# Values once per pixel, and key rows that rotate through six places: a change to an attention and convolution kernel

## The chip, the cores and the metric

The kernel runs on one core of one Trainium2 chip. The metric is the device time of one execution in microseconds (us). A core has a matrix engine (TensorE, PE in the profile), three engines for elementwise work (VectorE = DVE, ScalarE = ACT, GpSimd = POOL), and SyncE (SP), which issues most of the DMA transfers. Each engine works through its own list of instructions in order, and they meet at semaphores. On-chip memory is SBUF (128 partitions); TensorE writes to PSUM, in banks of 512 floats per partition, and another engine must copy a bank out before it is used again.

## The reference

Two layers over x of shape (2, 128, 256, 256), float32, NCHW, each added to its own input. `_gn` is a group norm with 32 groups over a whole image.

```python
x = x + attention(_gn(x))     # layer 0
x = x + conv_block(_gn(x))    # layer 1
# attention: windows of 8x8 queries, neighbourhoods of 12x12 keys and values
q, k, v = split(einsum('bchw,oc->bohw', x, W_qkv), 3)    # 4 heads of 32
k, v = unfold_windows(k), unfold_windows(v)              # padded by 2, step 8
attn = einsum('bnd,bmd->bnm', q * SCALE, k)
attn = softmax(attn + rel_pos_emb(q, rel_height, rel_width) + FIXED_MASK)
out = einsum('bnm,bmd->bnd', attn, v)                    # then W_out, 1x1
```

FIXED_MASK leaves only pairs of pixels whose relative position has one fixed parity in the rows and one in the columns. So a window falls into four classes (r, c) of row and column parity, in each of which 16 queries meet 6 x 6 = 36 keys, and no pair crosses between them. The conv block is a 5x1 convolution and a 3x1 depthwise one, times a dilated 1x3 projection to 8 channels.

## The kernel before, in words

**Tiling.** An image is 32 strips of 8 rows, and the strips of both images are counted k = 0 to 63. Layer 0 works in units u = 2k + r: the row parity r of strip k, 128 units. A unit covers 32 windows of one strip as 16 pairs of neighbours, both column parities c. For a pair and one (r, c), the keys are a block of 6 rows x 10 columns = 60 (two 6 x 6 neighbourhoods that overlap by two columns), on 60 of 64 partitions; c = 0 and c = 1 take the two halves of the 128.

**Order.** The order of each engine's list is written by hand: what the main loop calls in sequence is what TensorE, VectorE, ScalarE, GpSimd and SyncE each run in sequence. One unit is:

- SyncE: the rows of strip k+2 (`load_rows`, in even units), a load of later rows for the next image's group norm statistics (`load_next`, in odd units), and the unit's result rows (`f_x1`, in `project`, to DRAM).
- VectorE, in even units: `normalise(k + 1)`, which writes the normed rows (L343) into padded cells `xn` of 60 elements, together with what neighbours share: the last two rows of the strip before (L334, GpSimd) and the edge columns (L348, L349). In odd units: `input_stats`.
- GpSimd: `by_place` (L358) sorts the pixels of strip k+1 into `xq`, and `old_keys` (L369) moves the two key rows that two strips share from one key buffer to the other.
- TensorE: `biases` (L479), which writes relative position logits and the mask to the four score banks; `scores` (L495); `values` (L460), which projects one padded cell per product, 16 products a unit; `coefficients` for the next strip (L439); `attend` (L520); then, in even units, `keys` of two later units (L375), in odd ones `queries` of two later units (L414); and `project` (L375 again, f_py).
- ScalarE and VectorE copy out of PSUM: exponentials (L504), values (L466, eight copies a unit), coefficients (L448 and L452), keys (L388), queries (L420), and the division of `attend`.

A value product's 128 result rows are the 60 padded places of c = 0 and of c = 1, so that a bank can be copied straight to `vt`, the operand of `attend`. A pixel at a strip's or a pair's edge lies in more than one cell, and is projected for each.

**Buffers.** `ps_pj` has four PSUM banks, in rotation for all products but the scores. `xn` has two buffers, by strip; `kt` two for each r; `vt` has one; the result rows `x1` two; rows of x (`raw`) three, and the statistics loads (`sx`) one. Layer 1 begins when layer 0's last units end, and takes over its buffers.

## Time and profile before

| | us |
|---|---|
| median of 3 runs (lowest, highest) | 3065.4 (3065.05, 3065.92) |
| the profiled execution: its own time | 3064.28 |
| its span on the profiler | 3062.5 |
| busy: TensorE matmuls | 2954.8 |
| busy: VectorE | 2517.6 |
| busy: ScalarE | 1732.8 |
| busy: GpSimd | 654.4 |

The span is a little shorter than the execution's own time, by 1.8 us, which lies around it. The page gives busy time of each engine, the chain of work that ended last, and groups of instructions by line. A line of a group reads: line, engine, operation, what is written <- what is read, tile shapes and count, then busy time, mean length of one in ns, and idle time ahead with its releaser. A line of a timeline reads: start in us, length, engine, source line, operation; "x32" says that 32 instructions were merged into one line; what stands in square brackets is idle time ahead and who ended it. TensorE's records are pipelined: a mean length of one counts overlaps, and the time from one start to the next is the better measure.

### The profile page before, as it was taken

To read this page: it belongs to the slowest core of one execution; us is meant where nothing else is said; L and a number is where in the kernel's file an instruction comes from. 1 tells how busy PE (TensorE), PEld (TensorE's weight loads), DVE (VectorE), ACT (ScalarE), POOL (GpSimd) and SP (SyncE) were. 2 spreads that over 40 slices of the span, in tenths; PEclk is the share of its full clock that TensorE was granted. 3 is DMA by queue.
4 is the path that set the end of the run, shared out by engine and by line. 5 is a ranking of instruction groups with operands and counts; after the bars stand their busy time and mean duration, and the time that the engine had idled before them with its cause. 6 is when DMAs were issued, how large, how long until landed. Compare 5 with 4: busy or idle time off the path is not lost.

```text
span 3062.5 us, 116727 instructions
## 1 busy us (share of the span) xinstructions
PE 2954.8 (96%) x52100; PEld 2224.4 (73%) x52100; DVE 2517.6 (82%) x4107; ACT 1732.8 (57%) x2677; POOL 654.4 (21%) x1437
## 2 busy tenths in 40 slices
PE   0799999999999999999999999999999999999998
PEld 0688888888888888888888888884444444444443
DVE  8788888888888877777777777768999999999997
ACT  0455555555555656555555555556666665666664
POOL 2323232323232323232323232310000000000000
PEclk9999999999999999999999999999999999999999
DMA  9433333333333222222222222226888888888885
GB/s 393 176 123 123 116 116 113 116 113 117 113 116 113 85 72 89 72 89 72 89 72 89 72 89 72 86 84 160 214 219 218 215 210 220 215 218 218 219 216 157
DMA packets 137407, 434.88 MB, mean 142 GB/s; under 512 B 12992, under 2 KB 87744, under 8 KB 104640
## 3 DMA queue, kind: packets, MB, share of 16 engines
q1 hardware_dynamic: 127824, 361.24, 34.0%
q0 software_dynamic: 9072, 66.06, 11.8%
q8 instruction: 413, 6.77, 0.9%
q14 instruction: 98, 0.80, 0.1%
HBM read 284.65 MB, written 134.22 MB: 137 GB/s over the span
## 4 chain that ended last, share of the span: by engine, by line
PE 95%; DVE 0%; ACT 0%; POOL 0%; DMA 0%; issue 0%; SPq 0%; ACTq 0%
PE f_pv L460 16%; PE a_o L783 11%; PE a_e L783 11%; PE f_s L495 8%; PE f_o L520 8%; PE f_pq L414 8%; PE f_pk L375 8%; PE f_py L375 7%; PE f_pa L439 4%; PE f_s L479 4%; PE a_d L834 4%; PE b L876 2%; PE a_c L783 2%; PE g L763 2%; POOL f_xq L358 0%; DMA ident<-in_c_ident 0%
## 5 line engine op out<-in xcount | busy, mean ns | idle before, releaser
L466 DVE COPY f_vt<-f_pv 64x512 f32<-64x512 f32 x512 | 354.7, 695 | 289.3 <-ACT f_vt L466 289.3
L358 POOL COPY f_xq<-f_xn 128x128 f32<-128x128 f32 x1024 | 397.9, 440 | 697.5 <-DVE f_xn L343 669.9
L460 PE MATMUL f_pv<-f_wqkvT,f_xn 128*128 128x128 f32 x4096 | 491.3, 278 | 0.0
L460 PEld LDWEIGHTS f_pv<-f_wqkvT,f_xn 128*128 128x128 f32 x4096 | 466.9, 192 | 8.5
L504 ACT ACTIVATE f_p<-f_s 128x512 f32<-128x512 f32 x512 | 264.4, 603 | 320.4 <-PE f_s L495 320.4
L420 ACT ACTIVATE f_q<-f_pq,f_head 128x512 f32<-128x512 f32 x512 | 302.8, 703 | 139.6 <-PE f_pq L414 139.6
L466 ACT COPY f_vt<-f_pv 64x512 f32<-64x512 f32 x512 | 297.6, 583 | 117.3 <-PE f_pv L460 116.8
L858 ACT ACTIVATE t<-t,w 128x1024 f32<-128x1024 f32 x127 | 145.9, 1149 | 367.6 <-DVE t L851 362.8
L865 DVE SCALAR_TENSOR_TENSOR t<-t,w,t 128x1024 f32<-128x1024 f32 x254 | 325.8, 1283 | 7.4 <-ACT t L858 1.3
L495 PEld LDWEIGHTS f_s<-f_q,f_kt 64*64 64x64 f32 x16384 | 250.8, 135 | 49.9 <-issue 49.9
L495 PE MATMUL f_s<-f_q,f_kt 64*64 64x64 f32 x16384 | 268.5, 220 | 0.6 <-issue 0.6
L388 ACT COPY f_kt<-f_pk 128x512 f32<-128x512 f32 x256 | 154.5, 604 | 196.6 <-PE f_pk L375 196.6
L520 PE MATMUL f_o<-f_vt,f_p 128*32 128x66 f32 x16384 | 262.4, 222 | 0.2 <-issue 0.2
L894 POOL DMA_DIRECT2D y<-f_x x63 | 54.6, 866 | 916.0 <-DVE y L886 612.5
L520 PEld LDWEIGHTS f_o<-f_vt,f_p 128*32 128x32 f32 x16384 | 241.1, 110 | 9.2 <-issue 0.3
L783 PE MATMUL a_o<-xm,w1s 128*128 128x512 f32 x512 | 241.7, 593 | 3.8 <-ACT t L774 3.8
L375 PE MATMUL f_pk<-f_xn,f_wqkvT 128*128 128x128 f32 (+2 forms) x1256 | 244.2, 346 | 0.0
L375 PE MATMUL f_py<-f_ot,f_woT 128*128 128x256 f32 x1024 | 242.0, 379 | 0.9 <-DVE f_ot L538 0.9
L783 PE MATMUL a_e<-xm,w1s 128*128 128x512 f32 x512 | 240.7, 591 | 0.0
L414 PE MATMUL f_pq<-f_xq,f_wq_s 128*128 128x256 f32 (+1 forms) x1370 | 240.6, 331 | 0.0
L334 POOL COPY f_xn<-f_xn 128x1280 f32<-128x1280 f32 x62 | 87.1, 1404 | 717.2 <-PE f_pv L460 717.2
L414 PEld LDWEIGHTS f_pq<-f_xq,f_wq_s 128*128 128x128 f32 x1370 | 208.3, 191 | 22.6
(141 smaller groups left out, 4701.1 us busy)
## 6 DMA issues: line engine op xcount, KB each, us to landing
f_raw<-in_x SPq DMA_DIRECT2D x62, 1280.0 KB, 7.8
f_x<-f_x SPq DMA_DIRECT2D x128, 512.0 KB, 3.4
y<-f_x POOLq DMA_DIRECT2D x63, 1024.0 KB, 8.0
out<-y SPq DMA_DIRECT2D x63, 1024.0 KB
f_sx<-in_x SPq DMA_DIRECT2D x54, 1024.0 KB, 12.0
raw<-f_x SPq DMA_DIRECT2D x64, 640.0 KB, 6.8
raw<-f_x SPq DMA_DIRECT2D x62, 384.0 KB, 7.4
f_sx<-in_x SPq DMA_DIRECT2D x8, 1280.0 KB
```

Source lines behind the costliest of these rows:

```text
L358: nc.gpsimd.tensor_copy(xq[:, half, t2, :, :, c].rearrange("p t r n e -> p r t n e"), cells[:, :, 16 * half + c : 16 * half + 16 : 2, 1 + ...
L375: nc.tensor.matmul(dst[:, 512 * lo // last : 512 * hi // last], w, moving[:, n * lo // last : n * hi // last], start=True, stop=True,)
L388: nc.scalar.copy(cur[:, c, 1:129, 2:6], pk.rearrange("p (j i) -> p j i", i=4))
L414: nc.tensor.matmul(pq.rearrange("p (h n e t) -> p h t n e", h=2, n=8, e=2)[:, half, lo:hi], wq_s, xq[:, half, :, :, r, c].rearrange("p s t ...
L420: nc.scalar.activation(q[:, c, :, i], pq.rearrange("p (n x) -> p n x", n=NPAIR), AF.Copy, scale=head[:, i : i + 1],)
L460: nc.tensor.matmul(pv[:, P * n : P * n + P], xn[k % 2][:, r, 4 * j + n].rearrange("p c x -> p (c x)"), wvT, start=True, stop=True,)
L466: (nc.vector.tensor_copy if c else nc.scalar.copy)(vt[rows, 4 * j : 4 * j + 4, :, c, 0:32], pv[rows].rearrange("p (n h d) -> p n h d", n=4 ...
L495: nc.tensor.matmul(sc[g][n // 8][64 * c : 64 * c + 64, n % 8].rearrange("p i x -> p (i x)"), keys_k[rows, c, 48 * n : 48 * n + 64], qs[u][ ...
L504: nc.scalar.activation(pts[u][:, g, 8 * half : 8 * half + 8].rearrange("p n i x -> p (n i x)"), sc[g][half].rearrange("p n i x -> p (n i x ...
L520: nc.tensor.matmul(po[32 * h : 32 * h + 32, n - lo], p[:, h // 2, n, h % 2], vt[:, n, h], start=True, stop=True,)
L783: nc.tensor.matmul(pa[:, : n * W], w, rows, start=i == 0, stop=i == len(terms) - 1)
L865: nc.vector.scalar_tensor_tensor(t3[:, j : j + 4], t1[:, j + tap : j + tap + 4, :], w3[:, tap : tap + 1], t3[:, j : j + 4], ALU.mult, ALU.add,
```

## The change

A strip's values are projected once per pixel. `xn` now holds, for each pair, the 128 pixels of four rows of each parity (r, c, row i, column j), only the four rows that the strip brings new; a small `xo` keeps the row that the queries need besides. `values(k + 1, ...)` does all 16 pairs in two halves, one in each unit of strip k: two banks a unit, one copied out by ScalarE and one by VectorE, into `vn`, which has a single buffer, in pixel order.

`bring(r, ...)` then copies `vn` by DMA, on SyncE's queue, from SBUF to SBUF into key order in `vt[r]`: for each c and piece one copy of the strip's own pixels and two of the edge columns that go to the neighbouring pairs. Both calls stand in the odd unit, `bring(0)` after the values, `bring(1)` after `attend`. Strip 0 of an image has two further rows above (`top_values`, built like `values`, and `bring_top`), held in the buffer `sx`.

Keys and values keep the rows that two strips share in place. The six key rows have six slots, and a strip's four new ones overwrite the four oldest: slots 2 to 5, 0 to 3, then 4, 5, 0, 1, and again. In the third case (k mod 3 = 2) the run wraps and is two pieces. A row keeps its slot, so the table `hot` of `biases` has three phases, by k mod 3. `old_keys` goes; `beside` (GpSimd) copies the edge columns of the keys. `kt` and `vt` are one buffer for each r, and `x1` one in place of two.

The norm is done a unit earlier, in odd units for strip k+2, the statistics in even ones, `by_place` after the keys or queries. Queries read `xn` and `xo`. The products of keys, queries and projections are cut into pieces by the table `PIECES`, and the first three or four halves of `biases` are cut in two. In layer 1 the pixel buffers take over the place of `vn` (`pixel_buffers`).

The core of the diff ("..." stands for lines left out, among them the removed bodies):

```diff
...
-ONE, TWO, THREE = (0, 32), (0, 16, 32), (0, 16, 24, 32)
-XC = 131
+ONE, TWO, THREE, FOUR = (0, 16), (0, 8, 16), (0, 6, 11, 16), (0, 4, 8, 12, 16)
+NKEY = 60
+PIECES = {
+    0: (ONE, ONE, ONE, 0), 1: (ONE, ONE, TWO, 0), 60: (THREE, TWO, THREE, 1), 62: (TWO, TWO, TWO, 0),
+    64: (THREE, TWO, THREE, 1), 70: (THREE, TWO, THREE, 1),
+}
...
+        xt = [both.sb.tile([P, 12 * 260], F32, tag=f"x{i}", name=f"f_xn{i}") for i in range(2)]
+        xn = [t[:, 0:2048].rearrange("p (n r c i j) -> p n r c i j", n=NPAIR, r=2, c=2, i=4) for t in xt]
+        xo = [t[:, 2048:2560].rearrange("p (n r c j) -> p n r c j", n=NPAIR, r=2, c=2) for t in xt]
+        tops = {}
+        kt = [cst.tile([P, 2, NPAIR * NKEY + 4], F32, tag=f"f_kt{r}", name=f"f_kt{r}") for r in range(2)]
+        vt = [cst.tile([P, NPAIR, 2, HEADS, 33], F32, tag=f"f_vt{r}", name=f"f_vt{r}") for r in range(2)]
+        vn = both.sb.tile([P, NPAIR, HEADS, 33], F32, tag="vn", name="f_vn")
...
-        x1p = l0.enter_context(tc.tile_pool(name="f_x1", bufs=2))
+        x1p = l0.enter_context(tc.tile_pool(name="f_x1", bufs=1))
...
+        def pieces(u):
+            return PIECES.get(u, (THREE, TWO, THREE, 4 if u % 4 == 1 else 3))
...
+            for i in range(NS - 3):
+                n = 10 if i < 12 else 8
+                stats_at[2 * (b * NS + i) + 2] = b + 1, row, n
...
+            for i, u in enumerate((16, 28, 44, 58)):
...
+            norm_at[2 * (b * NS + NS - 2)] = st_x, b + 1, f"x{b + 1}"
+            norm_at[2 * ((b + 1) * NS + 3)] = st_y, b, f"y{b}"
...
+        def slots_of(k):
+            first = (4 * k + 2) % 6
+            return [(0, 4, first)] if first < 4 else [(0, 2, 4), (2, 2, 0)]
         def normalise(k):
...
+            cur = xn[k % 2]
+            rows = raws[k].rearrange("p (i r) (n j c) -> p r c n i j", r=2, n=NPAIR, c=2)
...
+                t = rawp.tile([P, 10, W], F32, tag="sx", name=f"f_top_{k}", bufs=1).rearrange("p a b -> p (a b)")
+                x = t[:, 0:1024].rearrange("p (n r c i j) -> p n r c i j", n=NPAIR, r=2, c=2, i=2)
+                v = t[:, 1024 : 1024 + 8 * HEADS * 33].rearrange("p (n h d) -> p n h d", n=8, h=HEADS)
...
+                tops[b] = t[:, 0:1024], x, v
+                for r in range(2):
+                    nc.vector.tensor_scalar(
+                        x[:, :, r, :, 1], rows[:, r, :, :, 0].rearrange("p c n j -> p n c j"), mean, rstd,
+                        ALU.subtract, ALU.mult,
+                    )
+                before = x[:, :, :, :, 1]
...
+                before = xn[(k + 1) % 2][:, :, :, :, 3]
+            nc.gpsimd.tensor_copy(
+                xo[k % 2].rearrange("p n r c j -> p n (r c) j"),
+                before.rearrange("p n r c j -> p n (r c) j"),
+            )
...
+                        cur[:, :, r, c, 0 : hi - 1], rows[:, r, c, :, 1:hi], mean, rstd,
...
         def by_place(k, columns):
...
+            lo, hi = columns
+            for half in range(2):
+                windows = slice(8 * half, 8 * half + 8)
+                for c in range(2):
+                    nc.gpsimd.tensor_copy(
+                        xq[:, half, lo:hi, 0, :, c].rearrange("p t r n e -> p r t n e"),
+                        xo[k % 2][:, windows, :, c].rearrange("p n r (e t) -> p r t n e", t=4)[:, :, lo:hi],
+                    )
+                    for t2 in range(lo, hi):
...
+                            xq[:, half, t2, 1:4, :, c].rearrange("p t r n e -> p r t n e"),
+                            xn[k % 2][:, windows, :, c, 0:3, t2:8:4].rearrange("p n r i e -> p r i n e"),
...
+        def by_window(r):
+            return kt[r][:, :, 0 : NPAIR * NKEY].rearrange("p c (n x) -> p c n x", x=NKEY)
+        def beside(r, slot, m):
+            keys_r, end = by_window(r), NPAIR - 1
+            for side, dst, src, j in ((0, slice(1, NPAIR), slice(0, end), 7), (1, slice(0, end), slice(1, NPAIR), 0)):
+                first = 48 + 2 * slot + side
+                nc.gpsimd.tensor_copy(
+                    keys_r[:, :, dst, first : first + 2 * m - 1 : 2],
+                    keys_r[:, :, src, 8 * slot + j : 8 * (slot + m) : 8],
+                )
         def keys(u, first=TWO, second=TWO):
...
+            keys_r = by_window(r)
             def part(c):
...
+                in_parts(second if c else first, pk, wkT, xn[k % 2][:, :, r, c].rearrange("p n i j -> p n (i j)"))
+                for i, m, slot in slots_of(k):
+                    nc.scalar.copy(
+                        keys_r[:, c, :, 8 * slot : 8 * (slot + m)],
+                        pk.rearrange("p (n x) -> p n x", n=NPAIR)[:, :, 8 * i : 8 * (i + m)],
+                    )
+                if c:
+                    for i, m, slot in slots_of(k):
+                        beside(r, slot, m)
             def top():
...
+                beside(r, slot, 2)
...
+        def queries(u, first=TWO, second=TWO):
...
             def part(c):
...
+                by_pair = pq.rearrange("p (n x) -> p n x", n=NPAIR)
...
+                nc.tensor.matmul(by_pair[:, :, 0:8], wq_s, xo[k % 2][:, :, r, c], start=True, stop=True)
...
+                        by_pair[:, lo:hi, 8:32], wq_s,
+                        xn[k % 2][:, lo:hi, r, c, 0:3].rearrange("p n i j -> p n (i j)"),
...
+                        q[:, c, :, i].rearrange("p n (j t) -> p n j t", t=4),
+                        pq.rearrange("p (n t j) -> p n j t", n=NPAIR, t=4), AF.Copy,
...
+        def values(k, groups):
+            for g in groups:
+                pv = ps_pj.tile([P, 512], F32, tag="pj", name=f"f_pv_{k}_{g}")
+                for n in range(4):
+                    nc.tensor.matmul(
+                        pv[:, P * n : P * n + P],
+                        xn[k % 2][:, 4 * g + n].rearrange("p r c i j -> p (r c i j)"),
+                        wvT, start=True, stop=True,
+                    )
+                (nc.vector.tensor_copy if g % 2 else nc.scalar.copy)(
+                    vn[:, 4 * g : 4 * g + 4, :, 0:32], pv.rearrange("p (n h d) -> p n h d", n=4, h=HEADS)
+                )
+        def top_values(b):
...
+        def bring(r, pieces):
+            end = NPAIR - 1
+            for c in range(2):
+                at, to = 32 * (2 * r + c), 64 * c
+                for i, m, slot in pieces:
+                    lo = at + 8 * i
+                    nc.sync.dma_start(
+                        vt[r][to + 8 * slot : to + 8 * (slot + m), :, c], vn[lo : lo + 8 * m]
+                    )
+                    first = to + 48 + 2 * slot
+                    nc.sync.dma_start(
+                        vt[r][first : first + 2 * m - 1 : 2, 1:NPAIR, c], vn[lo + 7 : lo + 8 * m : 8, 0:end]
+                    )
+                    nc.sync.dma_start(
+                        vt[r][first + 1 : first + 2 * m : 2, 0:end, c], vn[lo : lo + 8 * m - 7 : 8, 1:NPAIR]
+                    )
+        def bring_top(r, b):
+            v, slot = tops[b][2], 4 * NS * b % 6
+            for c in range(2):
+                for odd in range(2):
+                    lo, to = 64 * odd + 16 * (2 * r + c), 64 * c
+                    nc.sync.dma_start(
+                        vt[r][to + 8 * slot : to + 8 * slot + 16, odd:NPAIR:2, c], v[lo : lo + 16]
+                    )
+                    first = to + 48 + 2 * slot
+                    nc.sync.dma_start(
+                        vt[r][first : first + 3 : 2, odd + 1 : NPAIR : 2, c], v[lo + 7 : lo + 16 : 8, 0 : 8 - odd]
+                    )
+                    nc.sync.dma_start(
+                        vt[r][first + 1 : first + 4 : 2, 1 - odd : NPAIR - 1 : 2, c],
+                        v[lo : lo + 9 : 8, 1 - odd : 8],
+                    )
+        def biases(u, halves=0):
...
+            done = 0
...
+                            for lo, hi in ((0, 4), (4, 8)) if done < halves else ((0, 8),):
+                                nc.tensor.matmul(
+                                    sc[g][half][
+                                        64 * c : 64 * c + 64, lo:hi, :, 16 * e : 16 * e + 16
+                                    ].rearrange("p n i x -> p (n i) x"),
+                                    hot[rows, k % 3, e],
+                                    cfs[k][rows, e, r, c, lo:hi].rearrange("p n i x -> p n (i x)"),
+                                    start=e == 0 and lo == 0, stop=False, skip_group_check=True,
+                                )
+                            done += 1
         def scores(u):
...
+                            kt[r][rows, c, NKEY * n : NKEY * n + 64],
...
+                            vt[r][:, n, :, h], start=True, stop=True,
...
-                in_parts(TWO, py, woT, ots.pop((u, c)).rearrange("p (n x) -> p n x", n=NPAIR))
+                in_parts(pieces(u)[2], py, woT, ots.pop((u, c)).rearrange("p (n x) -> p n x", n=NPAIR))
...
         load_rows(0)
         load_rows(1)
-        load_next()
         weights.load()
         with tc.manual_schedule(engines=ORDERED):
             normalise(0)
-            by_place(0, range(4))
-            emit(keys(0, ONE, TWO))
+            emit(keys(0, ONE, ONE))
+            top_values(0)
+            bring_top(0, 0)
+            values(0, range(4))
+            for r in range(2):
+                bring(r, slots_of(0))
+            bring_top(1, 0)
+            by_place(0, (0, 4))
             coefficients(0, 0)
             coefficients(0, 1)
+            normalise(1)
+            by_place(1, (0, 2))
             for u in range(2):
-                emit(queries(u, TWO, TWO))
+                emit(queries(u, ONE, ONE))
             for u in range(NU):
                 k, r = divmod(u, 2)
                 b, s = divmod(k, NS)
...
                 if r == 0:
                     if k + 2 < NB * NS:
                         load_rows(k + 2)
-                    if more:
-                        normalise(k + 1)
+                elif k + 2 < NB * NS:
+                    normalise(k + 2)
                 if u in stats_at:
                     input_stats(u)
+                if u == 0 or u in stats_at:
                     load_next()
...
-                if more:
-                    by_place(k + 1, (2 * r, 2 * r + 1))
...
-                if later:
-                    old_keys(u + 1)
-                biases(u)
+                biases(u, pieces(u)[3])
                 scores(u)
...
-                for j in range(4):
-                    values(u, j)
+                if more:
+                    at_top = (k + 1) % NS == 0
+                    if at_top and r == 0:
+                        top_values(b + 1)
+                    values(k + 1, (2 * r, 2 * r + 1))
+                    if r == 1:
+                        bring(0, slots_of(k + 1))
...
                 attend(u)
+                if more:
+                    if at_top:
+                        bring_top(r, b + 1)
+                    if r == 1:
+                        bring(1, slots_of(k + 1))
...
                 turn(u)
...
                 if r == 0:
-                    top = s == 0 or (k + 1) % NS == 0
-                    if u == 0:
-                        emit(keys(1, ONE, ONE))
-                    else:
-                        emit(keys(u + 1, TWO if top else THREE))
+                    emit(keys(u + 1, pieces(u)[0], pieces(u)[0]))
                     if more:
-                        emit(keys(u + 2, ONE if u > 0 and top and s else TWO if top else THREE))
+                        emit(keys(u + 2, pieces(u)[0], pieces(u)[0]))
                 elif later:
-                    second = THREE if k % 4 else TWO
-                    emit(queries(u + 1, THREE, TWO) + queries(u + 2, THREE, second))
+                    emit(queries(u + 1, pieces(u)[1], pieces(u)[1]) + queries(u + 2, pieces(u)[1], pieces(u)[1]))
+                if more and r == 0:
+                    by_place(k + 1, (2, 4))
+                elif k + 2 < NB * NS:
+                    by_place(k + 2, (0, 2))
                 if u > 0:
                     result_stats(u - 1)
                 project(u)
...
         def rows_buffer(i):
...
+            t = both.sb.tile([P, 12 * 260], F32, tag=f"x{i}", name=f"xm{i}")
+            xn[i] = t.rearrange("p (r w) -> p r w", w=260)
...
+        by_pixel = []
+        def pixel_buffers():
...
```

## The prediction

> **What bounds the kernel now.** I read the page's busy shares and chain first, then one layer 0 unit on the timeline of each engine, then SyncE's queue and its landing times. Shares and chain:
>
> ```profile
> PE 2954.8 (96%) x52100; PEld 2224.4 (73%) x52100; DVE 2517.6 (82%) x4107; ACT 1732.8 (57%) x2677; POOL 654.4 (21%) x1437
> ...
> PE 95%; DVE 0%; ACT 0%; POOL 0%; DMA 0%; issue 0%; SPq 0%; ACTq 0%
> PE f_pv L460 16%; PE a_o L783 11%; PE a_e L783 11%; PE f_s L495 8%; PE f_o L520 8%; PE f_pq L414 8%; PE f_pk L375 8%; PE f_py L375 7%; PE f_pa L439 4%; PE f_s L479 4%; PE a_d L834 4%; PE b L876 2%; PE a_c L783 2%; PE g L763 2%; POOL f_xq L358 0%; DMA ident<-in_c_ident 0%
> ```
>
> TensorE is the end-setting engine almost everywhere, and its largest single line is the value product f_pv. Layer 0 runs from about 108 to 2070 us as 128 nearly equal units. One unit on TensorE (start, length, what), ending with the next unit's first line:
>
> ```profile
> 599.89 1.12 PE L479 MATMUL f_s<-f_cf,f_hot 32*64 32x256 f32 x32
> 600.94 2.10 PE L495 MATMUL f_s<-f_q,f_kt 64*64 64x64 f32 x128
> 602.97 3.84 PE L460 MATMUL f_pv<-f_wqkvT,f_xn 128*128 128x128 f32 x32
> 606.74 1.15 PE L439 MATMUL f_pa<-f_xq,f_wb 128*64 128x64 f32 x32
> 607.82 2.05 PE L520 MATMUL f_o<-f_vt,f_p 128*32 128x66 f32 x128
> 609.79 3.78 PE L375 MATMUL f_pk<-f_xn,f_wqkvT 128*128 128x256 f32 x20
> 613.42 1.89 PE L375 MATMUL f_py<-f_ot,f_woT 128*128 128x256 f32 x8
> 615.24 1.12 PE L479 MATMUL f_s<-f_cf,f_hot 32*64 32x256 f32 x32
> ```
>
> No gap: 15.35 us a unit, of which f_pv takes 606.74 - 602.97 = 3.77. The helpers of the same unit, ACT and DVE:
>
> ```profile
> 602.20 2.07 ACT L504 ACTIVATE f_p<-f_s 128x512 f32<-128x512 f32 x4 [1.82 <-PE f_s L495]
> 604.22 0.58 ACT L466 COPY f_vt<-f_pv 64x512 f32<-64x512 f32 x1
> 607.94 0.78 ACT L448 ACTIVATE f_cf<-f_pa,f_keep 128x512 f32<-128x512 f32 x1 [0.46 <-PE f_pa L439]
> ```
>
> ```profile
> 600.61 2.91 DVE L343 TENSOR_SCALAR f_xn<-f_raw,mean_x,rstd_x 128x512 f32<-128x512 f32 x4
> 604.84 0.69 DVE L466 COPY f_vt<-f_pv 64x512 f32<-64x512 f32 x1 [0.48 <-ACT f_vt L466]
> 608.75 0.81 DVE L452 TENSOR_SCALAR f_cf<-f_pa,f_keep 128x512 f32<-128x512 f32 x1 [0.54 <-ACT f_cf L448]
> ```
>
> The coefficient copy of DVE ends at 609.56, 0.23 us before the key product that takes over its bank (609.79): the chain of PSUM banks is nearly tight. SyncE issues about two DMAs a unit in layer 0. The nearest relatives of the new copies are layer 1's SBUF to SBUF ones (the last two lines: KB each, us from issue to landing):
>
> ```profile
> 2212.60 3.42 SPq L777 DMA_DIRECT2D t<-t4p  x5
> ```
>
> ```profile
> f_raw<-in_x SPq DMA_DIRECT2D x62, 1280.0 KB, 7.8
> f_x<-f_x SPq DMA_DIRECT2D x128, 512.0 KB, 3.4
> t<-t4p SPq DMA_DIRECT2D x189, 32.0 KB, 2.0
> ```
>
> Five in 3.42 us: 0.68 each, one after the other.
>
> [...] in the trace the copies with 16 partitions took 0.61 us of the queue and those with 8 took 0.72. [...]
>
> **The change, part by part.**
>
> *Values once per pixel.* Before: 4096 records of f_pv. After: 64 strips x 16 products x 2 records = 2048, and 2 x 8 x 2 = 32 for the top rows. 2016 records fewer at 3.77/32 = 0.118 us = 237.5 us less TensorE, all on the chain. A unit becomes 15.35 - 1.89 = 13.46 us. Within it (from its start, by the lines above): biases to 1.05, scores 3.08, values 4.97, coefficients 6.05, attend 8.02, keys or queries 11.65, project 13.46.
>
> *Piece sizes of keys, queries, projections and split biases.* The same columns in other cuts; two units with 20 and 22 records for keys and queries took 3.63 and 3.60 us. Nothing; ±0.1 us a unit, ±13 us.
>
> *Copies out of PSUM.* ACT loses four 0.58 and gains one of about 0.60 a unit; DVE loses four 0.69 and gains one, and loses both edge copies. Key copies become two in one strip of three (slots 4, 5, 0, 1), about 0.2 us more each. Hidden: ACT's five layer 0 groups on the page come to 1119 us, 8.7 a unit, and drop to about 7; DVE is busy 1537 us between 108 and 2070, 12.0 a unit, and drops to about 9.5, of 13.46.
>
> *POOL.* In a unit of parity 0 it now does, behind the last key copy (ACT follows the product by 0.25 us, 613.42 to 613.67 in this unit, and takes 0.6: 12.5), two edge copies of keys (L369's 0.39) and 12 copies of by_place at about 0.3 (L358's eight took 3.34, 0.42 each, with 128 elements; the new have 64 and 96). Done at 12.5 + 0.8 + 3.6 = 16.9, 3.4 into the next unit, whose coefficients want it at 4.97. Hidden by 1.6 us.
>
> *The norm a unit ahead.* Its 2.91 us of DVE move to parity 1, the input statistics to parity 0: each unit keeps one such block before its value copy at 5.1. The rows it reads are issued about one unit earlier and land in 7.8. Nothing.
>
> *SyncE's copies.* Each strip issues per parity r and column half c a main copy (32 partitions) and two edge copies (4 partitions): 6 DMAs for r = 0, 6 for r = 1. In strips with k mod 3 = 2 the six places wrap and each falls in two: 12 and 12. Those of r = 0 start in the unit of parity 1 once both value copies are done, at 5.9 (DVE: 4.97 + 0.25 + 0.69); those of r = 1 queue behind them (their own wait, attend at 8.02, is over by then). Next behind on SyncE: the store of x1, the next rows, the next statistics load. Who waits: vn is a single buffer, so the next unit's value copies on ACT and DVE wait until all landed. Nominal start 4.4. What lateness costs: after a copy that starts at S, ACT's coefficients end at S + 0.60 + 0.78, DVE's at S + 2.25, and the first key bank needs that at 8.02. So S may be 5.75 for nothing; beyond, TensorE stands still one for one.
>
> No trace row has these shapes. By L777's lines the mains cost 0.65 with the gap, the edge copies [...] 0.76; a load right behind the 512-run store took 0.62 against 0.33 elsewhere, and the new mains have 256 or 512 runs, so 0.1 more per group of three: 2.27. Plain strip: 4 groups, last issue at 5.9 + 9.1 - 0.76 = 14.2, landed 2.0 later at 16.2, which is 2.7 into the next unit: free. Wrapped strip: 8 groups, last issue at 5.9 + 18.2 - 0.76 = 23.3, landed 25.3, S = 11.8: 6.0 us lost. 21 such strips (2, 5, ... 62): **126 us**. Bounds: at 0.66 for every DMA S = 9.6, 3.9 each, 81 us; at 0.96 (the slowest repeated form, L696's reload at 0.91 and its gap) S = 16.5, 10.8 each, 226 us. With L298's 0.33 there is no stall at all, but that is one run per partition over 128 partitions.
>
> *Start and batch border.* Strip 0 needs 12 + 6 + 6 + 12 copies. If SyncE starts them at 101.6 (the first norm begins at 95.0, its top values are out 6.6 us later), the 24th lands at about 121.6; unit 0, begun near 111.5, wants its value copy by 111.5 + 5.75: 4.4 us. The third row load is then issued at 129 and lands 7.8 later, for a norm that unit 1 begins with: 2.9. Off these 2.4, since strip 0's own value products run while POOL still fills xq: 5 in all, an estimate. At strip 32 twelve top copies come between: 12 x 0.76 = 9, say 10.
>
> Sum on the profiled execution's own 3064.3 (span 3062.5): 3064.3 - 237.5 + 126 + 5 + 10 = 2967.8; the median of the runs lies 1.1 above: **2969 us**, 3.1% less.
>
> **Rivals.**
> *No new wait* (0.19): the queue issues at 0.5 or less, or the copies land sooner; 2843 us (the sum without the 126), up to 2924. For: plain loads take 0.33. Against: each SBUF to SBUF copy in the trace takes 0.6 to 0.7.
> *More is lost* (0.11): 8 to 10.6 us a wrapped strip, or POOL late: from 0.43 us per by_place copy its slack is gone, and each further 0.1 costs 12 x 0.1 x 63 = 76 us. 3011 to 3066. For: L358's page mean is 0.44; against: the new copies are smaller, and its spacing 0.42.
> *Slower than before* (0.13): SyncE's queue becomes the bound. It decides from 222/21 = 10.6 us a wrapped strip, about 0.95 us a DMA; at 1.05 S is 18.6, 12.8 us each, 270 in all, 3113 us. For: [...] single issues of 0.91 and 1.05 occur. Against: layer 1's short copies keep 0.61 to 0.72 through 64 strips.
> That the change doesn't do what it says: the changed program's SyncE list is 1067 rows longer, as counted from the code, and the value copies do wait on eight DMA counts there. Left out.
>
> **Numbers.** Forecast 0.57 (stall 3.9 to 8 us: 2924 to 3011). 0.2% is about what a measurement of this kernel can tell from no change (3059 to 3072). Faster: 0.57 + 0.19 + 0.09 of the third = 0.85; same 0.03; slower 0.12. The range 2850 to 3055 leaves out the slower rival, the top of the third case and the lowest 0.04.
>
> **What would show it.** Right: f_pv at 2080 records; plain units of 13.4 to 13.6 us; every sixth unit (parity 0, behind a wrapped strip) near 19.5 with TensorE idle before the second attend bank or the first key bank, released by ACT or DVE copies that waited for a DMA f_vt<-f_vn; SyncE solid for 17 to 19 us there. Wrong: equal units without gaps (no new wait); gaps before f_pa released by POOL (more lost); solid SyncE in plain strips too, gaps in every other unit (slower). The step most likely to fail is the 2.27 us per group.

## The result, and the profile after

The changed kernel took 3111.2 us (median of 4 runs, 3105.7 to 3113.3) against 3065.5 before: a ratio of 1.0146, with the 95% interval 1.0129 to 1.0164. It is slower; the forecast was 2969.

The page after: busy shares, then the chain that ended last.

```profile
PE 2822.5 (91%) x51778; PEld 2157.9 (69%) x51778; DVE 2165.6 (70%) x3601; ACT 1509.0 (49%) x2379; POOL 691.9 (22%) x2049
...
PE 79%; SPq 11%; issue 5%; DMA 2%; ACT 1%; DVE 1%; POOL 0%; ACTq 0%; POOLq 0%
```

TensorE is busy for 132 us less (2954.8 - 2822.5), but its share of the chain fell from 95 to 79%; SyncE's queue has 11%, and "issue", time in which TensorE waited for nothing that the profile shows, 5%. The waits of TensorE between 130 and 2000 us (who waited for whom, sum in us, times, longest):

```profile
PE f_o L604 <- ACT f_vn L499: 112.0, 20, 13.0
PE f_pk L381 <- issue: 32.9, 29, 2.3
PE f_pq L446 <- issue: 7.5, 10, 1.5
PE f_o L604 <- issue: 5.1, 8, 1.8
```

The first line is the wait for `vn` that was forecast, once in each wrapped strip (k mod 3 = 2) and longest at the border of the images. The other lines were not forecast. The kernel before has no wait at all in this stretch. One wrapped strip on TensorE, on the engines that free its PSUM bank, and on SyncE (start, length):

```profile
466.60 0.90 PE L604 MATMUL f_o<-f_vt,f_p 128*32 128x66 f32 x48
473.05 2.43 PE L604 MATMUL f_o<-f_vt,f_p 128*32 128x66 f32 x80 [5.55 <-ACT f_vn L499]
475.41 4.47 PE L381 MATMUL f_pk<-f_xn,f_wqkvT 128*128 128x192 f32 x24
479.71 1.90 PE L381 MATMUL f_py<-f_ot,f_woT 128*128 128x192 f32 x12
```

```profile
472.41 0.59 ACT L499 COPY f_vn<-f_pv 128x512 f32<-128x512 f32 x1 [7.58 <-DMA f_vt<-f_vn]
```

```profile
452.64 0.67 SPq L524 DMA_DIRECT2D f_vt<-f_vn  x1
453.36 0.72 SPq L528 DMA_DIRECT2D f_vt<-f_vn  x1
454.13 0.65 SPq L531 DMA_DIRECT2D f_vt<-f_vn  x1
...
469.49 0.62 SPq L531 DMA_DIRECT2D f_vt<-f_vn  x1
```

SyncE issues without a pause for 17.5 us, and the value copy starts 12.2 us into the even unit (460.26). Behind the wait, 24 key products take 4.47 us in place of 3.6. The windows of the same stretch show why (columns: window, its length, busy time of each engine, then the granted clock, DMA share, GB/s):

```profile
446.50:460.26 13.76, 13.76 (x381) 12.86 (x380) 9.61 (x21) 7.57 (x14) 7.83 (x25) 1.00 0.37 77
460.26:467.50 7.24, 7.24 (x263) 6.43 (x262) 3.85 (x7) 2.55 (x5) 0.00 (x0) 1.00 0.54 78
467.50:473.05 5.55, 0.00 (x1) 0.00 (x1) 0.63 (x1) 0.64 (x2) 0.00 (x0) 0.73 0.73 147
473.05:481.54 8.49, 8.49 (x116) 8.14 (x117) 5.97 (x13) 3.09 (x7) 1.94 (x8) 0.77 0.83 315
481.54:495.29 13.75, 13.75 (x380) 12.84 (x379) 9.60 (x21) 7.58 (x14) 7.81 (x24) 1.00 0.43 106
```

The clock record of the trace has half speed from 470.1 to 476.9 us, from 2.6 us into the wait of 5.55 us on to 3.9 us behind it. So the clock was 0.77 on average over the 8.49 us after the wait, in which 13.75 - 7.24 = 6.51 us of work were done: 2.0 us lost after the wait has ended. And the kind of gap that has no releaser, in a plain even unit:

```profile
410.94 3.20 PE L381 MATMUL f_pk<-f_xn,f_wqkvT 128*128 128x192 f32 x20
415.26 0.81 PE L381 MATMUL f_pk<-f_xn,f_wqkvT 128*128 128x160 f32 x4 [1.12 <-issue]
```

It falls inside one PSUM bank's products: same weights, same operand tile, nothing to wait for.

**The gaps lie on instruction blocks.** For every gap over 0.4 us between 130 and 2100 us, the list below has how many TensorE instructions (products and weight loads) had begun before its end, and when the last packet of the instruction queue had begun (on the page: `q8 instruction: 412, 6.75, 0.9%`, packets of 16,384 bytes). Five of the 69 gaps of the changed kernel:

```
gap ends at us, length, ahead of   instruction number mod 256   begin of the last 16 KB packet
415.3  1.12  f_pk                  194                          2.5 us earlier
444.3  1.09  f_pk                  193                          2.2 us earlier
509.2  2.32  f_pk                  193                          2.4 us earlier
587.8  0.41  f_pq                  193                          2.6 us earlier
473.0  5.55  f_o (wait for vn)     248                          4.1 us earlier
```

48 of the 69 gaps end at number 192 to 195 of 256, a median of about 2.4 us after an instruction packet begins; the other 21 wait for `vn` and have other numbers. 6.75 MB over the 105,133 instructions of TensorE recorded here are 64.2 bytes each, so a packet of 16,384 bytes holds 255 of them, and the gaps come back at one place of 256: a block here is 256 instructions. That TensorE stands at these places because the next block has not come is my reading; the trace shows the place, and a packet that began 2.2 to 2.6 us before TensorE resumed. A strip has about 1536 instructions in both kernels, six blocks, so the block ends keep their place from strip to strip.

Unit by unit (from first bias product to first bias product), an undisturbed unit takes 13.75 us, and the sum of what is over that is, in us (of the profiled execution, which differs from the median in the second column by up to 34 us; the first two units and the seven around the border of the images are left out):

| kernel | time, us | 20 wrapped units | 48 others, image 1 | 49 others, image 2 |
|---|---|---|---|---|
| the change | 3111.2 | 148 | 35 | 32 |
| loads_apart | 3091.0 | 136 | 32 | 28 |
| late_values | 3149.2 | 48 | 72 | 155 |
| whole_biases | 3194.2 | 139 | 99 | 75 |
| all_three | 3176.4 | 48 | 141 | 94 |
| keys_first | 3002.3 | 4 | 59 | 44 |
| keys_first_apart | 2986.9 | 4 | 46 | 46 |
| no_copies | 3042.5 | 45 | 77 | 40 |
| no_copies_even | 3031.6 | 41 | 39 | 83 |
| after_shift | 3050.0 | 154 | 10 | 1 |
| keys_first_shift | 2963.7 | 1 | 59 | 31 |
| rows_on_act | 3089.5 | 115 | 37 | 42 |

### The profile page after: what moved, and what is told of

It is laid out like the page before. It is cut to its first block, busy times and chain, and to the rows that moved or that the text cites. A ratio compares the mean times of both kernels' runs of the same rounds, so it can differ in the third digit from the quotient of the medians.

```text
span 3110.5 us, 117353 instructions
## 1 busy us (share of the span) xinstructions
PE 2822.5 (91%) x51778; PEld 2157.9 (69%) x51778; DVE 2165.6 (70%) x3601; ACT 1509.0 (49%) x2379; POOL 691.9 (22%) x2049
## 3 DMA queue, kind: packets, MB, share of 16 engines
q8 instruction: 412, 6.75, 0.9%
## 4 chain that ended last, share of the span: by engine, by line
PE 79%; SPq 11%; issue 5%; DMA 2%; ACT 1%; DVE 1%; POOL 0%; ACTq 0%; POOLq 0%
PE a_o L887 11%; PE a_e L887 10%; PE f_pk L381 8%; PE f_o L604 7%; PE f_s L579 7%; PE f_pv L494 7%; PE f_py L381 6%; PE f_s L563 4%; PE f_pq L446 4%; SPq L531 4%; PE a_d L938 3%; SPq L528 3%; SPq L524 3%; PE f_pa L472 3%; PE b L980 2%
## 5 line engine op out<-in xcount | busy, mean ns | idle before, releaser
L395 POOL COPY f_kt<-f_kt 128x60 f32<-128x60 f32 (+1 forms) x348 | 105.1, 338 | 1355.7 <-ACT f_kt L409 1308.6
L372 POOL COPY f_xq<-f_xn 128x96 f32<-128x96 f32 x1024 | 370.0, 390 | 6.6 <-DVE f_xn L355 6.6
L381 PE MATMUL f_pk<-f_xn,f_wqkvT 128*128 128x160 f32 (+3 forms) x1504 | 267.4, 333 | 34.9 <-issue 32.9
L409 ACT COPY f_kt<-f_pk 128x512 f32<-128x512 f32 (+1 forms) x340 | 155.0, 481 | 267.6 <-PE f_pk L381 267.3
L381 PEld LDWEIGHTS f_pk<-f_xn,f_wqkvT 128*128 128x128 f32 x1504 | 240.7, 203 | 52.6 <-issue 42.2
L638 DVE TENSOR_TENSOR f_x<-f_py,f_raw 128x512 f32<-128x512 f32 x256 | 173.7, 691 | 140.4 <-PE f_py L381 135.5
L494 PE MATMUL f_pv<-f_wqkvT,f_xn 128*128 128x128 f32 x2048 | 262.1, 281 | 0.0
L494 PEld LDWEIGHTS f_pv<-f_wqkvT,f_xn 128*128 128x128 f32 x2048 | 238.2, 191 | 8.3
L381 PE MATMUL f_py<-f_ot,f_woT 128*128 128x160 f32 (+2 forms) x1520 | 243.4, 310 | 0.0
L381 PEld LDWEIGHTS f_py<-f_ot,f_woT 128*128 128x128 f32 x1520 | 229.7, 190 | 1.8 <-issue 1.0
```

Of the source, the lines that this page charges most:

```text
L372: nc.gpsimd.tensor_copy(xq[:, half, t2, 1:4, :, c].rearrange("p t r n e -> p r t n e"), xn[k % 2][:, windows, :, c, 0:3, t2:8:4].rearrange ...
L381: nc.tensor.matmul(dst[:, 512 * lo // last : 512 * hi // last], w, moving[:, n * lo // last : n * hi // last], start=True, stop=True,)
L409: nc.scalar.copy(keys_r[:, c, :, 8 * slot : 8 * (slot + m)], pk.rearrange("p (n x) -> p n x", n=NPAIR)[:, :, 8 * i : 8 * (i + m)],)
L494: nc.tensor.matmul(pv[:, P * n : P * n + P], xn[k % 2][:, 4 * g + n].rearrange("p r c i j -> p (r c i j)"), wvT, start=True, stop=True,)
L638: nc.vector.tensor_tensor(x1[:, :, c:W:2], py.rearrange("p (m t) -> p t m", t=4), raws[k][:, r:8:2, c:W:2], ALU.add,)
```

## The experiments

**First: the wait, the loads, the cut biases.** My theories after the result: A, the wrapped strips lose the wait for `vn` and the half clock behind it; C, the gaps without a releaser are late instructions, because two loads of 1280 KB run at once; E, the cut biases cost time. All three edits are of the changed kernel.

late_values:

```diff
-                    values(k + 1, (2 * r, 2 * r + 1))
                     if r == 1:
+                        values(k + 1, (2, 3))
                         bring(0, slots_of(k + 1))
...
                         emit(keys(u + 2, pieces(u)[0], pieces(u)[0]))
+                        values(k + 1, (0, 1))
```

> The first half of the next strip's values moves, in even units, from before the coefficients to behind the keys: the copies to vn then come at about 12 us of the unit, behind the landing of the wrapped strip's copies (about 12). Theory A (the loss in every sixth unit is the value copies' wait for vn, 5.2 us each, and behind it 2.2 us of half clock on TensorE): the 20 wrapped units go from 21.2 to about 13.9 us, no half clock windows between 200 and 2000 us, and the time falls by about 150 us to 2950 to 2975. Rival B (SyncE's queue is the bound, and a copy that isn't waited for here is waited for by attend, by the rows or by the stores): 3070 or more, with the gaps elsewhere.

loads_apart:

```diff
-                if u == 0 or u in stats_at:
+                if u == 0 or u - 1 in stats_at:
                     load_next()
```

> The statistics load of the first image is issued at the start of odd units and no longer right behind the row load in even ones. Theory C (the gaps of 1.0 to 2.3 us in the key products, which no semaphore ends, are TensorE's instruction fetch, late because two loads of 1280 KB keep the DMA engines full for 8 us): in the first image the gaps in the even plain units go, 26 us less, 3085. Rival D (the gaps belong to the instruction stream itself, its length and where it is cut): nothing changes, 3108 to 3114.

whole_biases:

```diff
-                biases(u, pieces(u)[3])
+                biases(u)
```

> The bias products stay whole in every unit. Theory E (the cut of three or four of them costs 0.20 us a unit, 1.25 against 1.05 us from the first bias to the first score): 25 us less, 3086, plain odd units at 13.55. Rival (the cut costs nothing, and the 0.29 us over the forecast come from elsewhere): 3108 to 3114. If the fetch gaps hang on the length of the stream they move too, by up to 20 us either way.

all_three has the three edits.

> The three edits together. If the causes are independent: 3111 - 150 - 26 - 25 = 2910. If one of them only hides another (a fetch that is late anyway, a queue that is full anyway): 2930 to 3000.

Measured: 3149.2 (ratio to before 1.0261, 1.0230 to 1.0292), 3091.0 (1.0081, 1.0065 to 1.0098), 3194.2 (1.0394, 1.0352 to 1.0437), 3176.4 us (1.0372, 1.0353 to 1.0391). The wrapped units fell from 21.2 to 16.2 us in late_values, so A's wait is real, but the time rose: the others lost 160 us more. In whole_biases undisturbed odd units did fall, from 13.75 to 13.54 us, so the cut costs 0.21; yet the whole is 83 us slower. Its waits of TensorE show where:

```profile
PE f_o L604 <- issue: 95.5, 51, 5.0
PE f_o L604 <- ACT f_vn L499: 86.2, 17, 12.8
```

The gaps moved from keys into the attention products, and grew from 1 to up to 5 us. Without the cuts a strip has about 25 instructions fewer than 1536, so the block ends wander through the strip; the cuts are padding that pins them. In late_values scores and attention came closer together, and its strips are about 3 instructions shorter than the change's, so that its block ends wander too; what each of the two costs was not tested. all_three, for which 2910 to 3000 us had been expected, has the order of the one and the short list of the other. loads_apart gained 20 of the 26 us expected, but in the first image new gaps of about 0.6 us came in odd units, where the load now runs. So C was only a part.

**Second: another order, no copies, and the loads in the kernel before.** keys_first puts the keys of the same strip's second unit between scores and attention, where the values were:

```diff
                 scores(u)
+                if r == 0:
+                    emit(keys(u + 1, pieces(u)[0], pieces(u)[0]))
...
-                    emit(keys(u + 1, pieces(u)[0], pieces(u)[0]))
                     if more:
                         emit(keys(u + 2, pieces(u)[0], pieces(u)[0]))
+                        values(k + 1, (0, 1))
```

(and values(k + 1, (2, 3)) in odd units alone, as above.)

> As in late_values, but the keys of the same strip's second unit stand where the values stood, between scores and attend, and the values of even units behind the other keys, so that the dense stretches of TensorE's instruction stream (scores and attend, 256 instructions in 2.0 us each) stay 2 us apart and the count per strip stays. Theory F (TensorE takes its instructions in blocks of 256; a block that is used up in less time than its fetch takes beside the DMA traffic stops it): the wait for vn is gone as in late_values (148 us less), the gaps at block ends stay about those of the change (60 to 90 us in all): 2950 to 2985. Rival B (what is taken away as a wait comes back as another one): over 3060.

> keys_first and the statistics load in odd units: by theory F and the 20 us that loads_apart gained, 2930 to 2965. Rival: as above, or the loads meet the copies of odd units and give the 20 us back: 2955 to 2990.

no_copies returns at once from `bring` and `bring_top`: it leaves out all copies from `vn` to `vt`, and attention works on old values.

> All copies from vn to vt are left out (so attend works on vt as it was first filled; all other work is done). Theory F, with the copies' own traffic as a cause of late fetches: no wait for vn (160 us less with the start and the border), and in the second image no gaps at block ends (32 us less), while those of the first image stay, since both big loads still come together: about 2905 to 2925. If the gaps belong to the stream and not to the traffic, they stay in both images: 2940 to 2960.

before_loads_together, in the kernel before:

```diff
                         load_rows(k + 2)
+                    if u > 0 and u - 1 in stats_at:
+                        load_next()
...
                     input_stats(u)
-                    load_next()
```

> The kernel before, with the statistics load of the first image issued right behind the row load of the even unit before, as in the changed kernel; nothing else. Theory C: gaps without a semaphore on 256-instruction boundaries in even units of the first image, 29 x 0.5 to 1.2 us: 3080 to 3100. Rival (before leaves the fetch enough time, and only the new order or the copies make it late): 3063 to 3068.

Measured: keys_first 3002.3 us (0.9799, 0.9782 to 0.9815) and keys_first_apart 2986.9 (0.9749, 0.9733 to 0.9766), both faster than the kernel before, though 17 and 22 us above the ranges expected. The wrapped units are at 14.0 us, and TensorE's largest waits in keys_first have no vn among them:

```profile
PE f_pv L494 <- issue: 34.5, 39, 1.8
PE f_s L579 <- issue: 30.2, 18, 2.5
PE f_o L604 <- issue: 7.9, 10, 2.6
PE f_o L604 <- DVE f_vn L499: 5.4, 2, 2.9
```

no_copies missed by far: 3042.5 us (0.9931, 0.9914 to 0.9947), with 93.5 us of waits of f_o for "issue" though no copy ran. Its instruction list is 7 shorter per strip (the waits for the copies are gone), so its block ends wandered too. before_loads_together was 1.0000 (0.9991 to 1.0009): two large loads at once do nothing to the kernel before. So C falls as the whole cause: to keep the two loads apart gained 20 us in the changed kernel, and to put them together cost nothing in this one.

**Third: moving the block ends alone.** Repeating small products at the start of the program, where TensorE is idle for 80 us, moves every later block end and changes nothing else in the program:

```diff
-                nc.tensor.matmul(
-                    pg[:, : 2 * NREL], wq_nat[32 * h : 32 * h + 32, :],
+                for _ in range(14 + 1):
+                    nc.tensor.matmul(
+                        pg[:, : 2 * NREL], wq_nat[32 * h : 32 * h + 32, :],
...
```

(6 + 1 in before_shift. no_copies_even is no_copies with one more bias half cut in every unit.)

> no_copies, with two more bias halves cut per strip: the waits that went with the copies had made TensorE's list 7 instructions shorter per strip, and these give 8 back, so that the block boundaries stay where the changed kernel has them. Theory G (what the gaps cost is set first by where the 256-instruction boundaries fall in a strip): 0.4 to 0.6 us of gaps a strip, as no_copies had in its first strips, and the time 2905 to 2935. If the boundaries' place is not the cause of no_copies' gaps of 2 to 5 us: 3030 to 3050, as no_copies.

> The kernel before, with 24 small matrix products more at its very start, where TensorE is idle for 80 us: 96 instructions, so that every block boundary in layer 0 falls 96 instructions earlier in its strip. Nothing else. Theory G: the first boundary of a strip moves from about 236 to about 140 instructions, where no_copies and whole_biases lost 5 to 6 us a strip: 64 x 2 to 5 us, 3190 to 3390. Rival (the kernel before has little traffic and 5.2 us a block, and isn't sensitive): 3063 to 3070.

> The changed kernel with 56 small products more at its start, 224 instructions: the boundaries fall 32 instructions later in the strip than now (224 to 255 in place of 192 to 224, where the kernel before has them). Theory G: 0.1 to 0.5 us of gaps a strip in place of 0.9, 25 to 50 us less, 3060 to 3085; the wait for vn stays. Rival (what is left of the gaps comes from the traffic, wherever the boundary is): 3105 to 3118.

before_shift took 3142.6 us (1.0255, 1.0238 to 1.0272): the kernel before loses 77 us by 96 instructions that run in idle time. One of its odd units:

```profile
330.33 1.70 PE L521 MATMUL f_o<-f_vt,f_p 128*32 128x66 f32 x104
333.60 0.55 PE L521 MATMUL f_o<-f_vt,f_p 128*32 128x66 f32 x24 [1.57 <-issue]
```

The loss is less than the 125 us expected at least. The list of waits puts 44 us of it down to "issue" (77 waits), but the rest lies at the same places. Layer 0 of both kernels is the same list of instructions, so the times from one start to the next can be compared one by one: of the 76.6 us by which before_shift is longer there, 75.1 lie on one step in 256, the one to number 193.

after_shift took 3050.0 us (0.9938, 0.9916 to 0.9961), 61 less than the change, faster than the kernel before, and 10 under the range expected. Compared step by step with the change, 73.6 us went at the old block ends and 12.6 came at the new ones. What TensorE waits for is now the wait for `vn` and little else:

```profile
PE f_o L605 <- ACT f_vn L500: 114.9, 20, 12.8
PE f_o L605 <- issue: 3.7, 6, 1.0
PE f_s L580 <- issue: 0.7, 3, 0.4
```

Where two lists differ, each step to a number 193 can be set against the median of the steps between the same two kinds of instruction. So measured, the block ends of layer 0 cost nothing in the kernel before, 75 us in the change, 64 in loads_apart, 176 in whole_biases, 249 in late_values and 266 in all_three.

no_copies_even was a miss: 3031.6 us (0.9887, 0.9871 to 0.9904). It lies in the range named for the case that the block ends' place is not the cause, but it doesn't test that: its strip came out 1 to 2 instructions too long, and the ends wandered from about position 235 to 145. Its strips keep the order of the others (least at 224 and above), at a higher level. The gap at block ends per strip, by the number of instructions from an even unit's start to the first block end (kernels that keep the order of the change or of the kernel before):

```
position      kernel: mean gap per strip, us
  0 to  31    no_copies 0.4
 32 to 111    no_copies 2.2 to 2.9
112 to 159    whole_biases 5.1 to 6.6; no_copies 3.6 to 5.1; before_shift 0.7 to 0.9 (128 to 159)
192 to 223    the change 0.9; no_copies 0.5 to 0.7; no_copies_even 1.2 to 2.2
224 to 255    before 0.0; after_shift 0.0 to 0.1; no_copies 0.2 to 0.3; no_copies_even 0.7
```

**Last: both together, and the row load.**

> keys_first_apart with the 224 instructions at the start. By theory G the gaps at block ends of keys_first_apart (46, 46 and 60 us of excess over 13.75 us a unit in the two images and behind wrapped strips) shrink to those of after_shift (10, 1 and 0 us), and there is no wait for vn: 114 + 127 x 13.75 + 30 for border, start and rest + 1009 for layer 1 = 2899, range 2875 to 2925. If the order with the keys ahead has its own bad places at these boundaries: 2950 to 3000.

keys_first_shift is the fastest: 2963.7 us (0.9666, 0.9650 to 0.9682), 3.3% under the kernel before, but 39 us over the main range expected; it lies in the one named for bad places of this order's own. 20 odd units behind wrapped strips take 16.9 us. Against keys_first_apart, 88.6 us went at the old block ends, but 74.1 came at the new ones: this order loses 0.9 us a strip at positions 224 to 255, where after_shift loses 0.1 at most. A place that is good for one order need not be good for another. In the 20 odd units the row load is late, since it is issued behind 24 copies. rows_on_act sends the rows from strip 2 on by ScalarE's queue:

```diff
-            nc.sync.dma_start(t[:, 0:n, :], x[b, :, 8 * s : 8 * s + n, :])
+            queue = nc.sync if k < 2 else nc.scalar
+            queue.dma_start(t[:, 0:n, :], x[b, :, 8 * s : 8 * s + n, :])
```

> keys_first_shift, with the row loads from strip 2 on issued by ScalarE's queue and no longer behind the copies on SyncE's. Theory H (the 3 us that odd units behind wrapped strips lose there, at block ends, come from the row load: stuck behind 24 copies it starts 10 us late and meets the scores and the attention of the odd unit): those 20 units go from 16.9 to about 14.2 us, 55 us less in all, 2905 to 2930. Rival (the copies themselves, or TensorE's wait for the norm of rows that come late, which stays): 2955 to 2985.

Theory H held for the units it speaks of: 13.9 us. But the whole took 3089.5 us (1.0082, 1.0061 to 1.0102), since the wrapped units are back at 19.5. SyncE's waits, the row load on ScalarE's queue, then TensorE's list, in one of them:

```profile
SPq L526 <- DMA f_raw<-in_x: 8.7, 1, 8.7
```

```profile
457.09 0.34 ACTq L317 DMA_DIRECT2D f_raw<-in_x  x1
```

```profile
468.76 2.54 PE L606 MATMUL f_o<-f_vt,f_p 128*32 128x66 f32 x84 [6.15 <-DMA f_vt<-f_vn]
```

A copy on SyncE waited 8.7 us for a row load on another queue that it has no data in common with. In the trace of the change all 1848 DMAs on SyncE's queue raise eight counters in turn, and 1808 of them wait first for the counter that they will raise themselves: 103 at 454.13 us and again, eight DMAs later, at 460.11. Here the list of waits names the row load; my reading is that the two queues share the eight counters, and that the row load had the turn before this copy's on the same one. ScalarE issued it at 457.09, when SyncE had already waited for 1.5 us, and it landed at 464.2. A wait moved once more.

## Why the prediction was wrong

By its own steps, from the profiled execution (3112.3 us, forecast 2967.8). 127 units of 13.46 us would be 1709 us from the first unit's start to the last's; they took 1990. The 281 us between are, against 126 + 10 forecast for the wrapped strips and the border and a part of the 5 for the start:

- **Values once per pixel**: 2048 f_pv records and 32 for the top rows, as forecast. 16 of them take 1.98 us, not 1.89; 0.1 us a unit.
- **Piece sizes, "nothing; ±0.1 us a unit"**: wrong. The cut biases cost 0.21 (whole_biases). With the 0.1 above a unit is 13.75 instead of 13.46: 37 us. What the cuts do is not in the unit at all: they hold a strip at six blocks.
- **SyncE's copies**: the price was right. A group of three took 0.62 + 0.65 + 0.89 (medians) and three gaps of 0.05, 2.31 us, forecast 2.27; the value copy starts at 12.2 (forecast 11.8), the gap is 5.2 on the mean of the 20 units (forecast 6.0). It is shorter because the wait is another one than the sum had: TensorE stops ahead of the second attend bank, 7.2 us into the unit shown, and goes on when ScalarE's copy to `vn` ends, where the sum had the first key bank (8.02) wait for VectorE's coefficients.
- **"TensorE stands still one for one"**: wrong. The clock record has a half speed window of 3.4 or 6.8 us at each of these waits (13.7 at the border), which last from 3.7 us up, and none at the other 48 gaps, up to 2.3 us; the prediction had no half speed in it. So a wrapped unit costs 7.4 us, 148 in 20 units where 120 were forecast.
- **Start and border**: 15 us at the start (5.4 until unit 0 begins, 9.2 in the first two units) for 5, and 21 around the border for 16 with its wrapped strip. Small.
- **What no step and no rival had**: 68 us in the other units, of which after_shift, by moving block ends alone, takes 57.

The sum of what was missed, 37 + 28 + 10 + 5 + 68 = 148, is the difference of 144 to within 4 us. The rival "slower" named 3113 us, close to the result, but by 1.05 us a copy and a stall of 12.8; measured were 0.77 and 5.2. The number agrees by chance.

Shown by runs: the wait for `vn` (keys_first takes it away, 148 to 4 us), the cost of the cuts, and that the place of the block ends alone moves the changed kernel by 61 us and the kernel before by 77. Argued only: why a block comes late. The trace has no time of request. My estimate has two causes. One is data traffic; the instruction packets have a queue of their own here (q8, 412 packets), and how data would hold them up the trace doesn't show. The other is that scores or attention use up 256 instructions in 2.0 us (128 score products and as many weight loads, 461.51 to 463.54 us), less than the 2.2 to 2.6 us from the beginning of a packet to the end of a gap. The layer 0 blocks of all 15 traces, counted from number 193 to the next 192, go with both:

| the block took | blocks | followed by a loss of over 0.2 us |
|---|---|---|
| under 2.6 us | 641 | 68% |
| 3.5 to 4.5 us | 2057 | 25% |
| over 6.5 us | 863 | 1 block |

Short blocks came late without much data in the way: in no_copies_even 54 of 54 of those under 2.6 us lost time, with the DMA engines 5% busy over the last 3 us. Traffic counts too: among the 2057 that share was 60% ahead of a loss and 37% elsewhere, and in loads_apart, which moves loads alone, the block ends cost 12.6 us less than in the change, step by step. Neither is enough: in rows_on_act 65 of 67 blocks under 2.6 us lost nothing to speak of. What decides a single case stays open. How much the copies' traffic adds at the changed kernel's own block ends stays open, since both kernels without copies let the ends wander.

## What to carry to other kernels

When TensorE's list is long and dense, count its instructions per loop turn and see where the multiples of 256 fall: in the changed kernel 48 of 69 gaps ended at one place of 256, inside runs of independent products, and an edit that drops a few instructions or waits can cost more than the work it saves (whole_biases: 0.21 us saved in an undisturbed odd unit, 83 us more in all). So compare variants at several positions (pad in idle time), or the comparison measures the position; one position is not equally good for every order (224 to 255: 0.1 us a strip at most in after_shift, 0.9 in keys_first_shift). Price a stall of TensorE as long as those here (3.7 us and more) with what the slower clock costs after it (2.0 us behind the one shown); and before moving a DMA to another queue, ask which completion it will have to follow (8.7 us in rows_on_act).

## What the runs showed of the hardware that I had not expected

- TensorE resumes at fixed instruction numbers (193 or 194 of 256 in nearly all cases) in the changed kernel and in twelve variants, by kernel a median of 2.3 to 2.4 us after a 16,384-byte instruction packet begins.
- 96 instructions in idle time cost the kernel before 77 us; 224 gained the changed one 61. In the first case 75 us lie on one step in 256.
- An issue wait of 8.7 us on SyncE came from a load on ScalarE's queue.
